# A mixture-of-experts combine brought from a stage of its own into the loops of the next layer

## The chip, the cores and the metric

The kernel runs on one core of a Trainium2 chip. A core has a matrix engine (TensorE, "PE" in the profile, with its weight loads shown as "PEld"), and the engines VectorE (DVE), ScalarE (ACT) and GpSimd (POOL), each of which takes its own instructions in the order in which they were issued to it; SyncE (SP) mostly issues DMAs. The engines wait for each other through semaphores. The metric is the device time of one execution in microseconds (us).

## The reference, cut to what matters

Everything is float32. `x` has 4 sequences of 1024 tokens of 128 features, 4096 tokens in all. Six layers follow one another, each on a layer norm of `x` and added to `x`:

```python
x = x + 0.5 * moe(layernorm(x), wg, w1, b1, w2, b2)
x = x + mamba(layernorm(x), W_in, conv_w, conv_b, W_xproj, W_dt, b_dt, A_log, D, W_out)
x = x + 0.5 * moe(layernorm(x), wg, w1, b1, w2, b2)        # same weights
x = x + 0.5 * soft(layernorm(x), phi_w, phi_b, expert_w, expert_b)
x = x + gla(layernorm(x), Wq, Wk, Wv, Wo, Wf1, Wf2, Wg1, Wg2, norm_weight)
x = x + 0.5 * soft(layernorm(x), phi_w, phi_b, expert_w, expert_b)
```

The first two kinds of layer and the soft one are, in short:

```python
def moe(x):                       # 8 experts of 128 -> 512 -> 128, two of them per token, room for 1024 rows each
    gates_k, idx_k = top_k(softmax(x @ wg), 2); gates_k /= sum(gates_k)
    disp[idx_k, loc] = x          # loc: the token's place in its expert's queue; beyond 1024 it is dropped
    out = relu(disp @ w1 + b1) @ w2 + b2
    return sum_k gates_k * valid * out[idx_k, loc]

def mamba(x):                     # 256 channels, 16 states
    u, z = split(x @ W_in); uc = silu(causal_conv4(u))
    dt, B, C = split(uc @ W_xproj); delta = softplus(dt @ W_dt + b_dt)
    h_t = exp(delta * A) * h_{t-1} + delta * B * uc        # along the tokens of a sequence
    return ((sum_n h * C + uc * D) * silu(z)) @ W_out

def soft(x):                      # 64 experts x 32 slots
    logits = x @ phi.T + phi_b
    D, C = softmax(logits over slots), softmax(logits over experts)
    X = tanh(layernorm(sum_tokens D * x))
    return sum_{experts, slots} C * (X @ expert_w + expert_b)
```

## The kernel before, in words

`x` stays in SBUF for the whole kernel, as 32 tiles of 128 tokens by 128 features. The kernel is one instruction stream per engine. Inside the layers the loops are written under a manual schedule for PE, DVE, ACT and POOL: on each of these engines the instructions stand in exactly the order in which the code issues them. A generator that is stepped with `next` once per turn of a loop is how one piece of work is laid between the pieces of another. Pools of tiles set when a buffer may be filled again.

**Layer norms.** Statistics of four tiles (`ln_stats`, L121 to L123, DVE: eight small instructions and `rstd`, the variance plus epsilon), the power -0.5 (`ln_root`, L130, POOL), the product of minus mean and rstd (`nmr`, L133, DVE), and for each tile `ln_apply` (L143, ACT), which writes the normed tile `xn`.

**The MoE layers** (`moe_layer`, from L148) route the tokens, gather rows of `xn` for the experts in blocks of 512, run the two matmuls, add `b2` (`eo`, L393, DVE), and scatter the result rows into `y2_d` in DRAM by POOL's indirect DMAs (L352), with a small `spacer` memset (L412) between the last ones. Each of a token's two rows has a place of its own in `y2_d`. At the end, the *combine* (L421 to L436) brings them back: for each of eight groups of four tiles, two loads of 256 KB (L425, on SP's queue, three buffers `y`), four scalings by the first gate on ACT (L427), four multiply-adds by the second gate onto `x` on DVE (L431), and one DVE add of 128x512 (L435). `after(j)` is called for each group behind it: the statistics, the power and `nmr` of the next layer's norm.

**Before Mamba** `soft_weights` (L740 to L786) loads the soft layers' `phi`, folds it, and computes on the chip a `flag` that says whether the logits are bounded. Then `mamba_layer` loads its weights on ACT's DMA queue (L456 to L463), `cw` (the convolution's weights times `w_in`, DVE) last.

**Mamba's loop.** A sequence is worked in two halves of 512 tokens, eight halves in all. A half's `prologue` (a generator of 16 steps) norms its four tiles, transposes them (L499, copy L501), computes the convolution and the projections (`pu` L520, silu L531, `dbc` L543, `pd` L565), and softplus (ACT L570 to L575, `w`, `l`, `delta`, `du` on DVE L576 to L580). The loop then runs over 128 units, one for each half and state n; a unit fetches B and C of its state (`fetch`: `Cs` L595 and `Bs` L601 by SP's DMAs, or `pb` by a matmul, L607), multiplies `dBu` (`feed` L617, two units ahead, POOL for ten of the 16 states and DVE for the other six), takes `dA` (`decay` L625, ACT, two ahead), scans two channels' halves along the tokens (`scan` L635, DVE, `hst`), keeps the last column for the next half (`keep` L646, ACT), multiplies by C (`times_c` L651, POOL, `hc`), and sums over the states on PE (`sums` L666). The prologue of the half after the running one is stepped once per unit, from two units before the running half begins to its unit 13. The half before is ended by `epilogue`, stepped from unit 2 on (`zs` L673 DVE, `po` L678 PE, `x` L685 DVE, then the next norm's statistics).

**Before the soft layer** the second MoE's combine is followed by the run-time branch on `flag` (`values_load` L1572, `If` L1573); inside the taken side `phiM` (a copy of the folded `phi` on ACT, L1576, whose last row is set to -1 by a DMA, L1579) is made, and `soft_bounded` begins with a memset of `xT`'s last rows on POOL (L832, `xT` holds all normed tokens transposed).

**The soft layer's first loop** runs over 64 units, half of the 2048 slots by one tile of tokens each. `norm` and `turn`/`take` (L852 transposes into `pt`, which takes a buffer of the logits; L857 copy to `xT` by ACT) prepare the next four tiles, at units 0 to 3 and 4 of each eight. A unit computes logits `l` (L866, PE), their negated maximum `nmh` (L870, DVE), the exponential `ex` (L875, ACT), and one unit later sums and reciprocal (`sm` L882 and L883, DVE) and the weighted `dm` (L887, POOL), and three units later the spread `px` (L898, PE):

```python
for k in range(NK + CS * NB + XL + 3):
    if k < NK:
        logits(k); expo(k)
        g, r = divmod(k, 8)
        if 4 * (g + 1) < NT:
            if r < 4: norm(4 * (g + 1) + r)
            elif r == 4: turn(g + 1); take(g + 1)
    ...
    if 0 <= k - 1 < NK: total(k - 1); weigh(k - 1)
    if 0 <= k - LAG < NK: spread(k - LAG)
```

After this loop come the slots' own work (L924 to L962) and a second loop over combine weights (`clogits` L977 to `finish` L1033), whose `L` buffers come from the pool `lp` of 15.

## Time and profile before

| | us |
| --- | --- |
| median of 3 runs (lowest, highest) | 2390.34 (2389.11, 2394.69) |
| the profiled execution: its time, its span | 2391.2, 2389.1 |
| mean granted clock of PE in it | 0.903 |
| first MoE's last scatter; first loads of `y` | 269.35; 270.8 |
| first convolution matmul of Mamba | 313.1 |
| Mamba's loop, about (one half) | 344 to 889 (67.6) |
| second MoE's last scatter; first loads of `y` | 1157.4; 1158.8 |
| first soft layer's first logits; first `nmh` | 1200.07; 1203.89 |
| its first loop ends, about (eight units of it) | 1429 (28.54) |

The time of an execution is some 2 us above the span that the profile shows of it, and steps of the text are made against that one execution. In the profile's rows, a line number belongs to the code of that kernel; `out<-in` are the program's names; a group's row has the number of instructions, the busy time of all and the mean time of one in ns, and behind the second bar the idle time of that engine just ahead of them with what ended it. A line of the timeline has the start in us, the duration, the engine, the line, the instruction, and in square brackets how long the engine had been idle before it, and for whom it waited.

### The profile page before, as it was taken

Reading aid. Unit: us, or ns where it says so; the run is one execution under the profiler, and the core shown is the slowest. Engines: PE = TensorE matmul, PEld = TensorE weight load, DVE = VectorE, ACT = ScalarE, POOL = GpSimd, SP = SyncE. Lnnn points to the kernel's source line nnn. Section 1 sums busy time; section 2 is a strip of 40 time slices with the busy share of each in tenths; the row PEclk is TensorE's granted clock in tenths of the full one; section 3 lists DMA queues with packets and bytes.
Section 4 is the critical chain, followed back from the end, with each engine's and each line's share of the span. In section 5 each row is a group of like instructions: output and inputs, shape, how many; then the busy total and the mean of one; then the engine's idle time right before and its main releaser. Section 6 shows DMA issues by size and latency. Waiting matters only on the chain. (4 is left out here: it accounts for less than half of the span.)

```text
span 2389.1 us, 17980 instructions
## 1 busy us (share of the span) xinstructions
PE 1959.0 (82%) x5889; PEld 913.7 (38%) x5889; DVE 1391.7 (58%) x1947; ACT 924.2 (39%) x1453; POOL 1392.5 (58%) x898
## 2 busy tenths in 40 slices
PE   4667548899888874687389998999888799989998
PEld 3445313333333233454234444444222344434443
DVE  4211447878779774111477774556688677764444
ACT  3222346566446533222333334333344233334331
POOL 2666328888779881666345556666244355556663
PEclk9989868999978895789699999999898699999999
DMA  6111323232232324111200000000000000000000
GB/s 238 33 44 45 91 100 111 92 115 84 94 107 94 109 78 162 37 46 44 86 1 0 0 1 1 1 1 0 6 0 1 1 0 0 1 1 5 9 9 15
DMA packets 63677, 111.23 MB, mean 47 GB/s; under 512 B 7999, under 2 KB 41423, under 8 KB 58581
## 3 DMA queue, kind: packets, MB, share of 16 engines
q1 hardware_dynamic: 45062, 81.37, 10.3%
q0 software_dynamic: 8192, 16.79, 2.5%
q10 hardware_dynamic: 10322, 11.85, 1.5%
q8 instruction: 48, 0.79, 0.1%
q14 instruction: 53, 0.43, 0.1%
HBM read 90.53 MB, written 19.44 MB: 46 GB/s over the span
## 5 line engine op out<-in xcount | busy, mean ns | idle before, releaser
L887 POOL TENSOR_TENSOR dm<-ex,sm 128x1024 f32<-128x1024 f32 x128 | 244.7, 1913 | 218.2 <-DVE sm L883 125.1
L651 POOL TENSOR_TENSOR hc<-hst,Cs 128x1024 f32<-128x1024 f32 x128 | 278.1, 2183 | 89.8 <-DVE hst L635 41.8
L666 PE MATMUL py<-hc,ident 128*128 128x512 f32 x512 | 287.1, 697 | 38.3 <-POOL hc L651 28.3
L995 POOL TENSOR_TENSOR acc<-acc,L 128x1024 f32<-128x1024 f32 x96 | 226.0, 2354 | 114.4 <-ACT L L987 113.7
L987 ACT ACTIVATE L<-pl,pbc 128x512 f32<-128x512 f32 x256 | 162.1, 684 | 282.3 <-PE pl L977 277.8
L866 PE MATMUL l<-phiT,xT 128*128 128x512 f32 x512 | 246.6, 605 | 14.8 <-ACT xT L857 8.7
L875 ACT ACTIVATE ex<-l,nmh 128x1024 f32<-128x1024 f32 x128 | 142.8, 1115 | 285.4 <-DVE nmh L870 283.4
L977 PE MATMUL pl<-xT,phiM 128*128 128x512 f32 x512 | 242.2, 597 | 0.0
L1021 PE MATMUL py<-L,yt 128*128 128x512 f32 x512 | 238.4, 593 | 4.4 <-DVE L L1011 4.4
L898 PE MATMUL px<-dm,xn 128*128 128x512 f32 x512 | 240.8, 593 | 0.9 <-POOL dm L887 0.9
L870 DVE TENSOR_REDUCE nmh<-l 128x1 f32<-128x1024 f32 x128 | 156.5, 1223 | 107.9 <-PE l L866 107.9
L625 ACT ACTIVATE dA<-delta,A 128x512 f32<-128x512 f32 x256 | 178.4, 721 | 86.3 <-DVE hst L635 83.6
L617 POOL TENSOR_TENSOR dBu<-du,Bs 128x1024 f32<-128x1024 f32 x80 | 177.0, 2214 | 38.0 <-ACT dA L625 38.0
L378 ACT ACTIVATE hT<-ph,cols 128x512 f32<-128x512 f32 x128 | 84.2, 686 | 285.7 <-PE ph L374 166.8
L374 PE MATMUL ph<-dT,w 128*128 128x512 f32 x256 | 137.4, 655 | 69.1 <-ACT hT L378 58.3
L666 PEld LDWEIGHTS py<-hc,ident 128*128 128x128 f32 x512 | 100.9, 211 | 215.2 <-issue 131.2
L352 POOL DMA_INDIRECT y_d<-eo,dest x128 | 126.1, 985 | 92.7 <-DVE eo L393 61.8
L635 DVE TENSOR_TENSOR_SCAN hst<-dA,carry,dBu 128x512 f32<-128x512 f32 x128 | 154.6, 1262 | 5.4 <-POOL dBu L617 4.3
L882 DVE TENSOR_REDUCE sm<-ex 128x32 f32<-128x1024 f32 x128 | 154.7, 1209 | 0.0
L866 PEld LDWEIGHTS l<-phiT,xT 128*128 128x128 f32 x512 | 97.2, 193 | 145.9 <-issue 115.5
L635 DVE TENSOR_TENSOR_SCAN hst<-dA,dBu 128x512 f32<-128x512 f32 x128 | 146.9, 1202 | 6.9 <-ACT dA L625 3.6
L1011 DVE TENSOR_TENSOR L<-L,rd 128x1024 f32<-128x1024 f32 x128 | 147.0, 1211 | 0.1
(248 smaller groups left out, 2856.9 us busy)
## 6 DMA issues: line engine op xcount, KB each, us to landing
Cs<-bc_d SPq DMA_DIRECT2D x32, 1024.0 KB
Bs<-bc_d SPq DMA_DIRECT2D x80, 256.0 KB, 3.3
w<-in_w SPq DMA_DIRECT2D x4, 2048.0 KB
y<-y_d SPq DMA_DIRECT2D x32, 256.0 KB, 3.5
y_d<-zero SPq DMA_DIRECT2D x1, 4096.0 KB
ew<-in_ew ACTq DMA_DIRECT2D x1, 4096.0 KB
x<-in_x SPq DMA_DIRECT2D x8, 256.0 KB, 8.3
xn_da<-xn ACTq DMA_DIRECT2D x8, 256.0 KB, 14.7
```

What stands on the lines that cost most here:

```text
L617: eng.tensor_tensor(dBu, r["du"], r.pop(("B", n)).unsqueeze(2).to_broadcast([P, HB, NC]), ALU.mult,)
L625: nc.scalar.activation(dA, r["delta"][:, :, c], AF.Exp, scale=A[:, c * DS + n : c * DS + n + 1],)
L635: nc.vector.tensor_tensor_scan(hst[:, :, c], r.pop(("dA", n, c)), dBu[:, :, c], 0.0 if h == 0 else carry[b][:, c, n : n + 1], ALU.mult, AL ...
L651: nc.gpsimd.tensor_tensor(hc, r.pop(("h", n)), Cs.unsqueeze(2).to_broadcast([P, HB, NC]), ALU.mult)
L666: nc.tensor.matmul(r["py"][:, c, :], ident, hc[:, :, c], start=False, stop=(n == DS - 1))
L866: nc.tensor.matmul(l[:, q * 512 : (q + 1) * 512], xT[:, j * P : (j + 1) * P], phiN[:, o : o + 512], start=True, stop=True,)
L887: nc.gpsimd.tensor_tensor(dms[k], exs.pop(k), sms.pop(k).unsqueeze(2).to_broadcast([P, NG, PS]), ALU.mult,)
L898: nc.tensor.matmul(px[hf * 2 + q], xns[j // 4][:, j % 4, :], dmf[:, q * 512 : (q + 1) * 512], start=(j == 0), stop=(j == NT - 1),)
L977: nc.tensor.matmul(pl[:, i, :], phiM[:, (2 * c + i) * P : (2 * c + i + 1) * P], xT[:, t * TB : (t + 1) * TB], start=True, stop=True,)
L987: nc.scalar.activation(L[:, i, :], pl[:, i, :], AF.Exp, bias=pbc[:, 2 * c + i : 2 * c + i + 1], scale=-1.0,)
L995: nc.gpsimd.tensor_tensor(accs[t], accs[t], L, ALU.add)
L1021: nc.tensor.matmul(pys[t], yt[:, 2 * c + i, :], L[:, i, :], start=(c + i == 0), stop=(c == CS - 1 and i == 1),)
```

## The change

The combine is taken out of `moe_layer`. The gates are kept in two tiles of the whole kernel, and the combine of one group of four tiles becomes a generator of six steps: the two loads; ACT's four scalings; DVE's four multiply-adds and the add; the statistics; POOL's power; `nmr`. `ln_root` is split into the last two. The `y` buffers are two instead of three.

- For Mamba, group 0 is run ahead of the first prologue and group 1 behind it. From then on, at unit 3 of each of the first six halves, the group of the half after the next is begun (`k // 16 + 2`), and one step of it is issued at the head of each unit, ahead of the epilogue's step. So the loads are issued at unit 3, ACT's scalings at 4, DVE's part at 5, statistics at 6, the power at 7 and `nmr` at 8.
- For the first soft layer, group 0 runs ahead of the first norm and group 1 behind the first `take`; groups 2 to 7 are begun at `k % 8 == 1`, so the loads stand at the head of unit 1 of eight, the scalings at 2, DVE's part at 3, statistics at 4, the power at 5 and `nmr` at 6.
- The branch on `flag` now stands behind the second MoE's scatters and ahead of its combine, and `phiM` is made before the second MoE. On the side of the branch that isn't taken here, the combine runs as a plain loop.
- `lp` has 14 buffers instead of 15.

```diff
+    def ln_pow(ln, j0, n=4):
+        js = slice(j0, j0 + n)
+        nc.gpsimd.tensor_tensor(
+            ln[1][:, js], ln[1][:, js], half_t.to_broadcast([P, n]), ALU.pow
+        )
+
+    def ln_minus(ln, j0, n=4):
         mv, rstd, nmr = ln
         js = slice(j0, j0 + n)
-        nc.gpsimd.tensor_tensor(
-            rstd[:, js], rstd[:, js], half_t.to_broadcast([P, n]), ALU.pow
-        )
         nc.vector.scalar_tensor_tensor(
             nmr[:, js], mv[:, js, 0], -1.0, rstd[:, js], ALU.mult, ALU.mult
         )
+
+    def ln_root(ln, j0, n=4):
+        ln_pow(ln, j0, n)
+        ln_minus(ln, j0, n)
...
-    def moe_layer(w1, w2, b2, tag, ln, after):
+    def moe_layer(w1, w2, b2, tag, ln, gate):
...
-            gate = rp.tile([P, K, NT], F32, name="gate")
...
-                yp = s1.enter_context(tc.tile_pool(name=f"ey{tag}", bufs=3))
...
-                y_v = y2_d[: K * T, :].rearrange("(k j p) d -> p k j d", k=K, p=P)
-                for j in range(0, NT, 4):
...
-                    after(j)
...
+    def combine(yp, gate, j, ln):
...
+        y_v = y2_d[: K * T, :].rearrange("(k j p) d -> p k j d", k=K, p=P)
+        y = yp.tile([P, K, 4, D], F32, name="y")
+        for k in range(K):
+            nc.sync.dma_start(out=y[:, k, :, :], in_=y_v[:, k, j : j + 4, :])
+        yield
+        for i in range(4):
+            nc.scalar.activation(
+                y[:, 0, i, :], y[:, 0, i, :], AF.Copy,
+                scale=gate[:, 0, j + i : j + i + 1],
+            )
+        yield
+        for i in range(4):
+            nc.vector.scalar_tensor_tensor(
+                y[:, 1, i, :], y[:, 1, i, :], gate[:, 1, j + i : j + i + 1],
+                x[:, j + i, :], ALU.mult, ALU.add,
+            )
+        nc.vector.tensor_tensor(
+            x[:, j : j + 4, :], y[:, 0, :, :], y[:, 1, :, :], ALU.add
+        )
+        yield
+        ln_stats(ln, j)
+        yield
+        ln_pow(ln, j)
+        yield
+        ln_minus(ln, j)
+        yield
+
+    def run(pieces):
+        for _ in pieces:
+            pass
...
-    def mamba_layer(ln, ln_next):
+    def mamba_layer(ln, ln_next, before):
...
             with tc.manual_schedule(engines=ENGINES):
-
-                for _ in prologue(*halves[0], rs[0], psa, "dA"):
-                    pass
+                run(before(0))
+
+                run(prologue(*halves[0], rs[0], psa, "dA"))
+                run(before(NJ))
                 for k in range(3):
                     at(fetch, k)
...
-                ahead, behind = iter(()), iter(())
+                ahead, behind, first = iter(()), iter(()), iter(())
                 for k in range(-LEAD, len(units) + 7):
+                    if k % DS == 3 and (k // DS + 2) < len(rs):
+                        first = before((k // DS + 2) * NJ)
+                    if k >= 0:
+                        next(first, None)
                     if k % DS == DS - LEAD and (k + LEAD) // DS + 1 < len(rs):
                         i = (k + LEAD) // DS + 1
                         ahead = prologue(*halves[i], rs[i])
...
-    def soft_bounded(phiN, phiM, pbc, ew, eb, tag, ln, after=None, last=False):
+    def soft_bounded(phiN, phiM, pbc, ew, eb, tag, ln, before=None, after=None, last=False):
...
-            lp = s.enter_context(tc.tile_pool(name=f"slp{tag}", bufs=15))
+            lp = s.enter_context(tc.tile_pool(name=f"slp{tag}", bufs=14))
...
             with tc.manual_schedule(engines=ENGINES):
+                first = iter(())
+                if before:
+                    run(before(0))
                 for i in range(4):
                     norm(i)
                 turn(0)
                 take(0)
+                if before:
+                    run(before(4))
                 for k in range(NK + CS * NB + XL + 3):
+                    if before and k % 8 == 1 and (k // 8 + 2) * 4 < NT:
+                        first = before((k // 8 + 2) * 4)
+                    next(first, None)
                     if k < NK:
                         logits(k)
                         expo(k)
...
     lns = [ln_begin(i) for i in range(6)]
+    gates = [const.tile([P, K, NT], F32, name=f"gate{i}") for i in range(2)]
...
-    moe("a", lns[0], lambda j: ln_group(lns[1], j))
+    moe("a", lns[0], gates[0])
     spool = ctx.enter_context(tc.tile_pool(name="softw", bufs=1, side="right"))
     phiN, pbc, flag = soft_weights(spool)
-    mamba_layer(lns[1], lns[2])
+    with tc.tile_pool(name="ya", bufs=2) as yp:
+        mamba_layer(lns[1], lns[2], lambda j: combine(yp, gates[0], j, lns[1]))
...
     ew, eb = expert_weights(spool2)
+    phiM = spool2.tile([D, NS], F32, name="phiM")
+    nc.scalar.copy(phiM, phiN)
+    mone = spool2.tile([1, 512], F32, name="mone")
+    nc.vector.memset(mone, -1.0)
+    nc.sync.dma_start(
+        out=phiM[D - 1 : D, :].rearrange("o (r c) -> o r c", c=512),
+        in_=mone.unsqueeze(1).to_broadcast([1, NS // 512, 512]),
+    )
...
-    moe("b", lns[2], lambda j: ln_group(lns[3], j))
-
-    def rest(soft):
-        soft("a", lns[3], lambda j: ln_group(lns[4], j))
+    moe("b", lns[2], gates[1])
+
+    def behind_soft(soft):
         gla_layer(lns[4], lns[5])
...
     bounded = nc.values_load(flag, min_val=0, max_val=1)
     with tc.If(bounded > 0) as cmp:
-        with tc.tile_pool(name="softm", bufs=1) as pool:
-            phiM = pool.tile([D, NS], F32, name="phiM")
...
-            rest(lambda *a_, **k: soft_bounded(phiN, phiM, pbc, ew, eb, *a_, **k))
+        def soft(*a_, **k_):
+            soft_bounded(phiN, phiM, pbc, ew, eb, *a_, **k_)
+        with tc.tile_pool(name="yb", bufs=2) as yp:
+            soft("a", lns[3], lambda j: combine(yp, gates[1], j, lns[3]), after)
+        behind_soft(soft)
     with cmp.Else():
...
         nc.scalar.activation(phiN, phiN, AF.Copy, scale=-1.0)
-        rest(lambda *a_, **k: soft_layer(phiN, ew, eb, *a_, **k))
+        with tc.tile_pool(name="yc", bufs=2) as yp:
+            for j in range(0, NT, 4):
+                run(combine(yp, gates[1], j, lns[3]))
+        soft("a", lns[3], after=after)
+        behind_soft(soft)
```

More of the change, by code (lines that the diff above doesn't have):

```diff
@@ L125, in ln_stats @@
         )
-    def ln_root(ln, j0, n=4):
+    def ln_pow(ln, j0, n=4):
[4 more added lines that the diff above has]
+    def ln_minus(ln, j0, n=4):
         mv, rstd, nmr = ln
         js = slice(j0, j0 + n)
-        nc.gpsimd.tensor_tensor(
-            rstd[:, js], rstd[:, js], half_t.to_broadcast([P, n]), ALU.pow
-        )
         nc.vector.scalar_tensor_tensor(
@@ L418, in moe_layer @@
                             output(blk)
-                y_v = y2_d[: K * T, :].rearrange("(k j p) d -> p k j d", k=K, p=P)
-                for j in range(0, NT, 4):
-                    y = yp.tile([P, K, 4, D], F32, name="y")
-                    for k in range(K):
-                        nc.sync.dma_start(out=y[:, k, :, :], in_=y_v[:, k, j : j + 4, :])
-                    for i in range(4):
-                        nc.scalar.activation(
-                            y[:, 0, i, :], y[:, 0, i, :], AF.Copy,
-                            scale=gate[:, 0, j + i : j + i + 1],
-                        )
-                        nc.vector.scalar_tensor_tensor(
-                            y[:, 1, i, :], y[:, 1, i, :], gate[:, 1, j + i : j + i + 1],
-                            x[:, j + i, :], ALU.mult, ALU.add,
-                        )
-                    nc.vector.tensor_tensor(
-                        x[:, j : j + 4, :], y[:, 0, :, :], y[:, 1, :, :], ALU.add
-                    )
-                    after(j)
-    def mamba_layer(ln, ln_next):
+    def combine(yp, gate, j, ln):
[29 more added lines that the diff above has]
+    def mamba_layer(ln, ln_next, before):
         HB = 512
@@ L1536, in gla_layer, with moe @@
                     next(behind, None)
-    def moe(tag, ln, after):
+    def moe(tag, ln, gate):
         with ExitStack() as s:
@@ L1547, in moe @@
             )
-            moe_layer(w1, w2, b2, tag, ln, after)
+            moe_layer(w1, w2, b2, tag, ln, gate)
     lns = [ln_begin(i) for i in range(6)]
+    gates = [const.tile([P, K, NT], F32, name=f"gate{i}") for i in range(2)]
     for j in range(0, NT, 4):
         ln_group(lns[0], j)
-    moe("a", lns[0], lambda j: ln_group(lns[1], j))
+    moe("a", lns[0], gates[0])
     spool = ctx.enter_context(tc.tile_pool(name="softw", bufs=1, side="right"))
     phiN, pbc, flag = soft_weights(spool)
-    mamba_layer(lns[1], lns[2])
+    with tc.tile_pool(name="ya", bufs=2) as yp:
+        mamba_layer(lns[1], lns[2], lambda j: combine(yp, gates[0], j, lns[1]))
     spool2 = ctx.enter_context(tc.tile_pool(name="softw2", bufs=1, side="right"))
     ew, eb = expert_weights(spool2)
+    phiM = spool2.tile([D, NS], F32, name="phiM")
[6 more added lines that the diff above has]
+    )
     for j in range(0, NT, 16):
         ln_root(lns[2], j, 16)
-    moe("b", lns[2], lambda j: ln_group(lns[3], j))
-    def rest(soft):
-        soft("a", lns[3], lambda j: ln_group(lns[4], j))
+    moe("b", lns[2], gates[1])
+    def behind_soft(soft):
         gla_layer(lns[4], lns[5])
@@ L1570, in rest, with after, soft @@
         soft("b", lns[5], last=True)
+    def after(j):
+        ln_group(lns[4], j)
     bounded = nc.values_load(flag, min_val=0, max_val=1)
     with tc.If(bounded > 0) as cmp:
-        with tc.tile_pool(name="softm", bufs=1) as pool:
-            phiM = pool.tile([D, NS], F32, name="phiM")
-            nc.scalar.copy(phiM, phiN)
-            mone = pool.tile([1, 512], F32, name="mone")
-            nc.vector.memset(mone, -1.0)
-            nc.sync.dma_start(
-                out=phiM[D - 1 : D, :].rearrange("o (r c) -> o r c", c=512),
-                in_=mone.unsqueeze(1).to_broadcast([1, NS // 512, 512]),
-            )
-            rest(lambda *a_, **k: soft_bounded(phiN, phiM, pbc, ew, eb, *a_, **k))
+        def soft(*a_, **k_):
[3 more added lines that the diff above has]
+        behind_soft(soft)
     with cmp.Else():
+        def soft(*a_, **k_):
+            soft_layer(phiN, ew, eb, *a_, **k_)
         nc.scalar.activation(phiN, phiN, AF.Copy, scale=-1.0)
-        rest(lambda *a_, **k: soft_layer(phiN, ew, eb, *a_, **k))
+        with tc.tile_pool(name="yc", bufs=2) as yp:
[3 more added lines that the diff above has]
+        behind_soft(soft)
 def kernel(**inputs):
```

## The prediction

> **What bounds the kernel now.** I read the summary first, then busy time by stretches around the four places that the change touches, then the instructions there in order of time, engine by engine, and last the grouped DVE rows of Mamba's loop.
>
> ```profile
> span 2389.1 us, 17980 instructions
> PE 1959.0 (82%) x5889; PEld 913.7 (38%) x5889; DVE 1391.7 (58%) x1947; ACT 924.2 (39%) x1453; POOL 1392.5 (58%) x898
> ...
> 264.00:306.00 42.00, 8.64 (x19) 3.34 (x19) 28.98 (x128) 14.53 (x42) 12.68 (x16) 0.68 0.38 107
> 480.00:550.00 70.00, 61.14 (x131) 23.03 (x131) 56.32 (x56) 42.55 (x74) 58.72 (x30) 0.91 0.29 102
> 1158.00:1200.00 42.00, 1.58 (x4) 0.73 (x4) 26.87 (x123) 14.22 (x38) 12.28 (x9) 0.50 0.35 101
> 1200.00:1300.00 100.00, 97.83 (x229) 42.60 (x230) 73.89 (x82) 38.76 (x48) 50.13 (x27) 0.98 0.00 1
> ```
>
> The columns of a stretch are its length, the busy time of PE, PE's weight loads, DVE, ACT and POOL, the granted clock, and DMA. The shares of the whole run hide the point: in the two stretches of 42 us PE does almost nothing, and the experts' results are combined, on DVE. In Mamba's loop (480 to 550) PE, DVE and POOL are all near 80 to 90%, so none is free. In the soft layer's first loop PE is full and DVE has a quarter of its time left.
>
> Mamba's loop, DVE and then ACT, where the pieces will land:
>
> ```profile
> 500.33 1.22 DVE L617 TENSOR_TENSOR dBu<-du,pb 128x1024 f32<-128x1024 f32 x1 [6.34 <-PE pb L607]
> 501.47 0.68 DVE L685 TENSOR_TENSOR x<-x,po 128x512 f32<-128x512 f32 x1
> 502.06 2.33 DVE L635 TENSOR_TENSOR_SCAN hst<-dA,dBu 128x512 f32<-128x512 f32 x2
> ...
> 506.58 2.32 DVE L635 TENSOR_TENSOR_SCAN hst<-dA,dBu 128x512 f32<-128x512 f32 x2
> ...
> 508.93 0.19 ACT L646 COPY carry<-hst 128x2 f32<-128x2 f32 x1 [2.26 <-DVE hst L635]
> ...
> 531.62 1.77 DVE L576 SCALAR_TENSOR_TENSOR w<-w,e 128x1024 f32<-128x1024 f32 x1 [4.20 <-ACT l L575]
> ```
>
> DVE waits 6.34 us for PE, then runs without a gap up to the scan that ends at 508.9; ACT waits for that scan and is then busy almost without a gap up to `l`, for which DVE waits again. So what is put on DVE between 501.5 and 506.6 lengthens the half.
>
> The soft loop, at the one unit in eight that transposes the next four tiles:
>
> ```profile
> 1242.04 0.35 DVE L883 RECIPROCAL sm<-sm 128x32 f32<-128x32 f32 x1
> 1242.89 0.60 PE L852 MATMUL pt<-ident,xn 128*128 128x128 f32 x4
> 1243.09 1.22 DVE L870 TENSOR_REDUCE nmh<-l 128x1 f32<-128x1024 f32 x1 [0.70 <-PE l L866]
> 1244.41 1.11 ACT L875 ACTIVATE ex<-l,nmh 128x1024 f32<-128x1024 f32 x1 [1.94 <-DVE nmh L870]
> 1245.58 1.98 PE L866 MATMUL l<-phiT,xT 128*128 128x512 f32 x4 [0.37 <-ACT ex L875]
> ```
>
> `pt` takes one of the two buffers of `l`, so the next logits wait for this unit's `ex`: PE has no slack here (it already waits 0.37), and DVE has 0.70 us.
>
> Grouped DVE rows of Mamba's loop, mean ns after the comma:
>
> ```profile
> L579 DVE TENSOR_TENSOR delta<-delta,l 128x1024 f32<-128x1024 f32 x8 | 22.4, 2802 | 0.3
> L576 DVE SCALAR_TENSOR_TENSOR w<-w,e 128x1024 f32<-128x1024 f32 x7 | 17.3, 2473 | 20.9 <-ACT l L575 20.9
> L123 DVE TENSOR_SCALAR rstd<-mv 128x4 f32<-128x4 f32 x7 | 6.6, 949 | 0.2
> L133 DVE SCALAR_TENSOR_TENSOR nmr<-mv,rstd 128x16 f32<-128x16 f32 x1 | 2.1, 2097 | 2.7 <-POOL rstd L130 2.7
> ```
>
> Alone (POOL idle) the first two take 1.23 us, the last two 0.16. Beside a POOL tensor operation they take up to 3.1 us, and the POOL one 2.9 to 3.1 instead of 2.13; one of the two stands until the other ends. Operations with one operand in PSUM (L617, L685), scans and statistics keep their time.
>
> **The change part by part.** Sums are made against the profiled execution, 2391.2 us (span 2389.1 and 2.1 around it); the median of the runs is 2390.34, 0.9 lower.
>
> *First combine taken out.* Before, Mamba's first convolution matmul starts at 313.1, behind all eight groups and then the load of `cw`. After, `w_in` and `cw` are issued on ACT's queue before any combine and land under the fold of phi. DVE is through with the fold at 275.2; the rest of the flag and `cw` 2.5, four L431 1.14, the add 0.69, four statistics pairs 1.67 (their length in Mamba's loop), rstd 0.16, pow 1.07, nmr 0.16 end at 282.7; xn, transposes and copy, about 2.9 as at 1191.7, give 285.6. That is -27.5. The second group now stands between the prologue's `du` and the first feed: 1.14 + 0.69 + 1.67 + 0.16 + 1.07 + 0.16 + 0.1 of gaps = 5.0; the next half's xn, which leads PE there, waited 1.4 before, so +3.7. POOL's first dBu is queued right behind that pow and starts before nmr: +2.1 (0 if it does not block). **-21.7.**
>
> *Six pieces in Mamba's loop* (halves 0 to 5). The DMA pair lies early in SP's order and lands in 3.5 us, ACT's four scalings (1.28) lie where ACT waits 4.9 us for PE; if that cover went, 1.28 per half. On DVE, behind the feed at 500.33: four L431 until 502.6, by when POOL's hc (502.42, 2.13) is waiting; the add goes behind it and ends at 505.4 instead of 503.2. The scan of state 5 is 3.85 late. Statistics 1.67; the first rstd waits for hc of state 5 (510.4); the second statistics were there before. The scan of state 6 ends at 514.5, not 508.85: 5.65 late, and with it ACT's chain to `l`. POOL's pow (1.04) fits, because POOL waits for that scan. Half 0 has a wait of 1.13 of ACT for `pd` in the chain, so 4.4. 5 x 5.65 + 4.4 = **+32.7.** Without blocking it is 1.83 + 1.67 + 0.16 = 3.66 per half, 22.0; those are the two ends.
>
> *Second combine taken out.* First nmh at 1203.89. After: loads land at 1161.7 and 1162.5 as now, DVE's add ends at 1164.4, statistics, rstd, pow, nmr 1168.0, xn and transposes 1170.1, copy 1170.8; the memset of xT (3.51), which held that copy until 1199.4, now runs behind the last scatter. The second group's add waits for ACT's scaling behind the copy (1172.1) and ends the group at 1176.2; nmh of unit 0 follows. **-27.7.**
>
> *Six pieces in the soft loop.* Unit 3 of eight: four L431 and the add, 1.83, with POOL's dm (1.91) let in between: 3.9, less the idle 0.70. Unit 4: statistics 1.67, rstd behind dm 2.2 in all, less 0.70. nmh is 4.7 late, the logits of unit 5 too, and PE has nothing to make it up with: 6 x 4.73 = **+28.4.** Without blocking 6 x 2.26 = 13.6.
>
> *The rest, at nothing.* The branch: between pow and the memset that followed it POOL lost 0.1 us, DVE 0.7; it now lies in the 2.8 us wait for the first load. phiM's copy (1.88 on ACT) moves to where ACT waits 9.56 us for the load of `ew`; if that cover went, 1.9. 14 instead of 15 `L` buffers: the mix that frees a buffer stands ahead of the logits that refill it in PE's own order anyway. On SP the loads of y stand in front of Bs loads, waiting for a DVE add that is over well before those buffers are free; if not, a dBu comes 3.3 late.
>
> The sum is -21.7 + 32.7 - 27.7 + 28.4 = +11.7: 2402.9 for a profiled execution, 2402 for the median.
>
> [...]
>
> **The rivals.**
>
> 1. *Faster: POOL doesn't get in between.* If DVE's operations follow each other too closely, only their own length counts: -23.8 + 22.0 - 27.7 + 13.6 = -15.9, 2374. For it: back to back, L431 overlap by 0.06. Against it: the add depends on the last of them, and between the dependent L578 and L579 POOL did get in (3.03 for L579).
> 2. *One loop blocks, the other not*: -3.1 or -1.1, 2387 to 2389.
> 3. *All hidden*: -23.8 - 27.7 = -51.5, 2339. DVE's idle shares speak for it, the two chains above against it.
> 4. *Much slower: PE's clock drops in each soft wait.* After a wait of 4.36 us in Mamba's loop four matmuls took 3.62 instead of 1.72; at 1200 about ten ran at half speed. 4 to 10 matmuls at 0.43 more, six times: +10 to +26, 2412 to 2428. It decides if the two waits join to more than about 4 us.
>
> That the pieces are not in the loops is excluded: the built order of the queues has them there.
>
> **How the numbers follow.** My forecast 0.50, rival 1 0.15, rival 2 0.15, rival 3 0.05, rival 4 0.15. Within 0.3% is 7.2 us, about what a measurement of this kernel can tell. The forecast's own range is 2394 to 2410, so a fifth of it is "same"; rival 2 nearly all; rivals 1 and 3 are faster, 4 slower: faster 0.23, same 0.22, slower 0.55. The range 2374 to 2420 leaves out rival 3 and the far halves of 1 and 4, some 0.2. A fast and a slow side both hold much; the two entries (each within 3 us) are surer than the two loops.
>
> **What would show it.** The first convolution matmul near 286 and soft's first nmh near 1176 less what Mamba gives back; halves 0 to 5 of Mamba 4 to 6 us longer each, 6 and 7 unchanged; the combine's add and rstd in the loops at 1 to 3 us; a wait of PE for `ex` of 2 to 5 us once per eight soft units, six times; soft b and the GLA layer unchanged. I am wrong if the halves keep their length, or if the add takes 0.7 us in the loops.

## The result, and the profile after

The changed kernel takes 2419.78 us (median of 4 runs, 2414.93 to 2423.44), the kernel before 2392.52 in the runs beside it: ratio 1.0109, 95% interval 1.0089 to 1.0130. Run again on another occasion it took 2417.67 against 2390.66, ratio 1.0115 (1.0098 to 1.0132). So it is 27 us slower; 2402 was forecast, and the range ended at 2420. The profiled execution took 2423.4.

The summary, and the same four stretches as before (columns as there):

```profile
span 2421.4 us, 17953 instructions
PE 1981.6 (82%) x5889; PEld 920.4 (38%) x5889; DVE 1429.8 (59%) x1947; ACT 922.0 (38%) x1453; POOL 1389.6 (57%) x898
...
264.00:306.00 42.00, 23.51 (x45) 9.33 (x46) 12.24 (x37) 12.24 (x23) 5.57 (x11) 0.78 0.24 68
480.00:550.00 70.00, 58.59 (x123) 22.33 (x122) 56.15 (x65) 37.80 (x67) 53.54 (x27) 0.89 0.33 106
1158.00:1200.00 42.00, 24.26 (x131) 16.98 (x130) 10.45 (x31) 12.53 (x25) 21.73 (x33) 0.79 0.21 63
1200.00:1300.00 100.00, 86.94 (x193) 36.69 (x192) 79.67 (x123) 36.12 (x51) 46.39 (x26) 0.94 0.07 21
```

The first of the two stretches in which PE did almost nothing is filled (8.64 us busy became 23.51). The third row of the four, 1158 to 1200, isn't the same stage any more: Mamba's loop is longer, so the second MoE still runs there, up to 1184.3. The idle stretch itself, from the end of the last scatter to the first `nmh`, has shrunk instead, from 46.52 us to 18.27 (before, then after):

```profile
1157.37:1203.89 46.52, 5.40 (x9) 2.49 (x10) 26.87 (x123) 14.24 (x38) 12.28 (x9) 0.50 0.32 92
```

```profile
1184.30:1202.57 18.27, 6.48 (x10) 2.92 (x11) 7.26 (x30) 4.68 (x13) 5.56 (x4) 0.50 0.40 118
```

In their place PE lost 11 of 100 us in the soft loop, and the three busy engines of Mamba's loop all have a little less work in 70 us: the loop runs slower.

By stages, read off the starts of a few instructions (the last scatter of each MoE layer, Mamba's first scan, its last `zs`, the first `nmh`, the first clamp `xs` of the slots, and the last add onto `x`):

| us | before, two profiles | changed, two profiles | difference of the means | forecast |
| --- | --- | --- | --- | --- |
| first MoE's last scatter to Mamba's first scan | 78.7, 80.7 | 63.0, 62.9 | -16.8 | -21.7 |
| first scan to Mamba's last `zs` | 541.9, 542.0 | 580.6, 574.5 | +35.6 | +32.7 |
| from there to the second MoE's last scatter | 267.4, 269.0 | 271.0, 272.1 | +3.4 | 0 |
| from there to the first `nmh` | 47.5, 46.2 | 19.2, 19.2 | -27.6 | -27.7 |
| from there to the first `xs` (soft loop) | 231.9, 231.7 | 264.4, 263.3 | +32.1 | +28.4 |
| from there to the last add onto `x` | 948.5, 948.0 | 949.6, 949.3 | +1.2 | 0 |

The sum of the differences is +27.9. Seven profiles with the changed order in Mamba's loop, those of the experiments among them, lie between 571.9 and 583.6 for its row, so a few us between two such profiles say nothing in that row.

Mamba's loop in the changed kernel, in order of time, the same half as in the fence of before:

```profile
500.88 1.22 DVE L637 TENSOR_TENSOR dBu<-du,pb 128x1024 f32<-128x1024 f32 x1 [6.34 <-PE pb L627]
502.02 1.14 DVE L440 SCALAR_TENSOR_TENSOR y<-y,gate,x 128x128 f32<-128x128 f32 x4
502.97 2.16 POOL L671 TENSOR_TENSOR hc<-hst,Cs 128x1024 f32<-128x1024 f32 x1 [6.40 <-PE py L686]
503.24 2.43 DVE L444 TENSOR_TENSOR x<-y 128x512 f32<-128x512 f32 x1
505.60 0.67 DVE L705 TENSOR_TENSOR x<-x,po 128x512 f32<-128x512 f32 x1
...
506.42 2.04 PE L546 MATMUL pu<-xT,w_in 128*128 128x512 f32 x2 [3.58 <-DVE x L705]
...
511.94 1.18 DVE L123 TENSOR_SCALAR rstd<-mv 128x4 f32<-128x4 f32 x1
513.04 2.32 DVE L655 TENSOR_TENSOR_SCAN hst<-dA,dBu 128x512 f32<-128x512 f32 x2
...
515.39 0.19 ACT L666 COPY carry<-hst 128x2 f32<-128x2 f32 x1 [3.08 <-DVE hst L655]
...
518.64 1.12 DVE L136 SCALAR_TENSOR_TENSOR nmr<-mv,rstd 128x4 f32<-128x4 f32 x1
...
538.07 1.61 DVE L596 SCALAR_TENSOR_TENSOR w<-w,e 128x1024 f32<-128x1024 f32 x1 [4.36 <-ACT l L595]
```

The feed is 0.55 late against before. `hc` slips in ahead of the add, which ends at 505.67; `carry`, which ACT does at the end of the scan of state 6, comes at 515.39 instead of 508.93, 5.9 us later after those 0.55, and `w` is 5.9 later too. Of the detail, the first `rstd` was not held (0.17 us), the second was (1.18); `nmr` was held for 1 us; and PE waited 3.58 us for the late `x` at 506.42, because `po` holds the buffer of the next `pu`; the two matmuls behind that wait took 2.04 instead of 1.10.

The grouped DVE rows of the loop (344 to 890 us), mean ns after the comma:

```profile
L596 DVE SCALAR_TENSOR_TENSOR w<-w,e 128x1024 f32<-128x1024 f32 x7 | 24.2, 3454 | 25.0 <-ACT l L595 25.0
L444 DVE TENSOR_TENSOR x<-y 128x512 f32<-128x512 f32 x6 | 14.6, 2436 | 0.5
L123 DVE TENSOR_SCALAR rstd<-mv 128x4 f32<-128x4 f32 x13 | 11.3, 872 | 0.5
L136 DVE SCALAR_TENSOR_TENSOR nmr<-mv,rstd 128x4 f32<-128x4 f32 x6 | 5.4, 905 | 0.0
```

All six adds took 2.4 us, where one alone takes 0.69. And `w`, a bystander, rose from 2473 to 3454 ns, presumably because a half that is later meets POOL's work at another point; no run separates that.

The soft loop, the units 3 to 5 of eight (their lines of before are in the prediction):

```profile
1242.16 2.69 DVE L440 SCALAR_TENSOR_TENSOR y<-y,gate,x 128x128 f32<-128x128 f32 x4
1242.38 2.06 POOL L912 TENSOR_TENSOR dm<-ex,sm 128x1024 f32<-128x1024 f32 x1 [1.52 <-ACT xn L150]
1244.94 0.69 DVE L444 TENSOR_TENSOR x<-y 128x512 f32<-128x512 f32 x1
1245.55 1.22 DVE L895 TENSOR_REDUCE nmh<-l 128x1 f32<-128x1024 f32 x1
1246.86 1.11 ACT L900 ACTIVATE ex<-l,nmh 128x1024 f32<-128x1024 f32 x1 [4.55 <-DVE nmh L895]
1248.03 0.71 PE L877 MATMUL pt<-ident,xn 128*128 128x128 f32 x4 [1.70 <-ACT ex L900]
...
1252.74 2.90 PE L891 MATMUL l<-phiT,xT 128*128 128x512 f32 x4 [2.29 <-ACT ex L900]
...
1255.69 1.23 DVE L895 TENSOR_REDUCE nmh<-l 128x1 f32<-128x1024 f32 x1 [2.69 <-PE l L891]
```

`dm` gets in among the four multiply-adds, which take 2.69 us instead of 1.14; `nmh` is late, `pt` waits 1.70 for `ex`, the next logits 2.29, and then run slowly, 2.90 us for four instead of 1.98. Eight units, counted from one `pt` to the next, take 34.13 us where that happens and 28.54 before.

The slow matmuls are PE's clock. In the profiles of before and of the changed kernel the granted clock is either 1.00 or 0.50, and every stretch at one of the two, but the last, is 3.41 us long or a whole multiple of that. In this soft loop it is at 0.50 for one such slot in each turn, from 1216.12, 1253.66, 1287.80, 1321.93, 1356.06 and 1390.20. Three slots around the turn above in this profile, and four around a turn of the second profile with the same two waits (1.70 and 2.29 us, ending at 1243.89 and 1248.60); the clock is the third number from the end of a row:

```profile
1246.83:1250.25 3.42, 2.22 (x8) 1.05 (x8) 3.21 (x11) 1.50 (x2) 1.83 (x1) 1.00 0.51 147
1250.25:1253.66 3.41, 1.12 (x3) 0.49 (x3) 2.71 (x4) 1.59 (x2) 0.60 (x2) 1.00 0.01 2
1253.66:1257.07 3.41, 3.41 (x5) 1.33 (x4) 1.38 (x2) 0.06 (x1) 2.35 (x2) 0.50 0.00 0
```

```profile
1240.72:1244.13 3.41, 1.71 (x6) 0.63 (x5) 3.30 (x5) 1.41 (x2) 0.00 (x0) 1.00 0.40 118
1244.13:1247.55 3.42, 2.18 (x8) 0.81 (x6) 3.25 (x12) 0.20 (x2) 1.91 (x1) 1.00 0.12 36
1247.55:1250.96 3.41, 2.36 (x6) 1.16 (x7) 1.61 (x3) 1.48 (x2) 1.96 (x2) 1.00 0.01 2
1250.96:1254.37 3.41, 3.41 (x10) 1.50 (x9) 2.70 (x5) 1.12 (x1) 1.78 (x2) 1.00 0.00 0
```

In the first, the whole second wait lies in one slot, in which PE is idle for 2.29 us, and the next slot runs at 0.50. In the second, an edge at 1247.55 cuts that wait in two, no slot is idle for more than 1.70, and the clock stays at 1.00: from that `pt` eight units take 32.44 us. So the second wait alone was enough where it lay within one slot, and was not where an edge cut it. In the soft loop of the first profile a slot at 0.50 followed on each of the six slots with 2.29 to 2.89 us of idle PE and on none with 1.32 or less; in that of before no slot had more than 1.53, and from 1204.29 on the clock was 1.00. The changed kernel's low slots come in all six turns of the one profile and in five of the other; the first turn, with a wait of 3.16 us, is one of them.

At Mamba's entry, SP's queue before and then after:

```profile
270.82 3.24 SPq L425 DMA_DIRECT2D y<-y_d  x6
275.35 0.34 SPq L785 DMA_DIRECT2D pb_d<-pb  x1
```

```profile
276.75 0.34 SPq L810 DMA_DIRECT2D pb_d<-pb  x1
278.21 0.28 SPq L811 DMA_DIRECT2D phiT<-pb_d  x1
278.70 7.04 SPq L431 DMA_DIRECT2D y<-y_d  x6
...
281.81 1.28 ACT L434 ACTIVATE y<-y,gate 128x128 f32<-128x128 f32 x4 [5.08 <-DMA y<-y_d]
```

The first loads of `y` used to be issued ahead of the two small DMAs of the fold of `phi`. Now they stand behind them, and those wait for the fold: 8 us later, 278.70 instead of 270.82.

### The profile page after: what moved, and what is told of

Same layout as the page of the kernel before. It is cut to its first block, busy times and chain, and to the rows that moved or that the text cites. A ratio compares the mean times of both kernels' runs of the same rounds, so it can differ in the third digit from the quotient of the medians.

```text
span 2421.4 us, 17953 instructions
## 1 busy us (share of the span) xinstructions
PE 1981.6 (82%) x5889; PEld 920.4 (38%) x5889; DVE 1429.8 (59%) x1947; ACT 922.0 (38%) x1453; POOL 1389.6 (57%) x898
## 5 line engine op out<-in xcount | busy, mean ns | idle before, releaser
L923 PE MATMUL px<-dm,xn 128*128 128x512 f32 x512 | 246.6, 604 | 0.4 <-POOL dm L912 0.4
```

The source lines that it names most:

```text
L923: nc.tensor.matmul(px[hf * 2 + q], xns[j // 4][:, j % 4, :], dmf[:, q * 512 : (q + 1) * 512], start=(j == 0), stop=(j == NT - 1),)
```

## The experiments

Each kernel is the changed one with the edit shown. Times compare with the kernel before run beside it on the same chip; that took about 2390 us on some occasions and about 2338 on others (on record, chips 0 and 2 for the first, 6 and 1 for the second, each on one occasion). In the profiles that difference lies in the two MoE layers, some 30 us in each (for instance 242 instead of 271 us from Mamba's last `zs` to the second MoE's last scatter); what makes it was not tried. The entries and the soft loop are alike within 1 or 2 us where the code is the same, and are compared across; Mamba's loop in the changed order spreads as said above.

**One part at a time.** The second combine as one stage again:

```diff
+    with tc.tile_pool(name="yb", bufs=3) as yp:
+        for j in range(0, NT, 4):
+            run(combine(yp, gates[1], j, lns[3]))
...
-            soft("a", lns[3], lambda j: combine(yp, gates[1], j, lns[3]), after)
+        soft("a", lns[3], after=after)
```

> Only the first combine is in pieces (Mamba's loop); the second is one stage again ahead of the branch, as before. Theory 'two independent bills': the profile of the changed kernel, read by stages, gave Mamba's entry -15.4 us, its eight halves +38.6, the second MoE +3.7, the soft entry -28.3 and the soft loop +32.6. Undoing the second part must then leave -15.4 + 38.6 = +23 us against the kernel before (2413 to 2418; +27 if the second MoE's 3.7 belong to the copy of phi, which this kernel keeps early). Rival 'shared cause' (the branch's place, 14 buffers, or the early phi copy make a good part of the loss): the time stays within 5 us of the changed kernel's 2420 although the soft loop is as before.

And the first one as one stage again:

```diff
     moe("a", lns[0], gates[0])
+    with tc.tile_pool(name="ya", bufs=3) as yp:
+        for j in range(0, NT, 4):
+            run(combine(yp, gates[0], j, lns[1]))
...
-        mamba_layer(lns[1], lns[2], lambda j: combine(yp, gates[0], j, lns[1]))
+    mamba_layer(lns[1], lns[2], lambda j: iter(()))
```

> Only the second combine is in pieces (soft layer's loop); the first is one stage again. Two independent bills: soft entry -28.3, soft loop +32.6, so +4 us against before, +8 with the second MoE's 3.7: 2394 to 2402, and Mamba's halves 67 to 69 us again. Rival 'shared cause': more than +15 us. The half of Mamba that took 77.4 us in the profile of before, at a clock of 0.82, decides another thing: if it is there in this profile too, it is a property of the order of before, if not, of that one execution.

Mamba's part alone: 2357.84 against 2337.09, +20.8 where +23 was expected, ratio 1.0096 (1.0073 to 1.0118); the soft stages are back at 46.5 and 232.8. This kernel keeps the 14 `L` buffers, so they cost 1.0 us at most in that loop. The soft part alone: 2351.62, +14.5, ratio 1.0062 (1.0041 to 1.0083), where 4 to 8 was expected. The excess is at Mamba's entry, which took 88.0 us, 8.3 more than the 79.7 of before: in this kernel the fold of `phi` doesn't run beside the combine as it did before, but behind it (its matmuls start at 273.93, 4 us behind the last add of the combine). So its one-stage entry is not that of before; without those 8.3 it is +6.2. The two bills then make 20.8 + 6.2 = 27.0, and no sign of a shared cause is left.

**Before and changed, profiled on one chip.**

> The kernel before, for a profile on the chip of the other runs. Two points are open. Half 4 of Mamba: 77.4 us in the profile of before and 77.4 to 78.7 in every other one, so it is expected at 77 again (a property of the program); if it comes out at 68, the profile of before was a single bad draw and the loop's bill is 9 us higher than read. The second MoE, from Mamba's last zs to its last scatter: 241 to 243 in the four kernels that copy phi early, on that chip. Theory 'the copy of phi delays it by 3.7': 237 to 239 here. Rival 'drift of the DMAs': 240 to 243 here too.

> The changed kernel against the kernel before on the chip of the other runs. The four kernels run so far give, in differences to before: first part alone +20.8, second part alone +14.5 (of which 9.2 is its one stage entry, which stands worse than before's), so the two bills say 20.8 + 14.5 - 9.2 = +26 us. Rival (the parts interact): more than 5 us away from that.

The first took 2389.85. Half 4 of Mamba takes 77.5 us again, its neighbours 68: it is a property of that order, and that half has room for a piece (77.5 and 78.7 in the changed kernel, where the halves 1, 2, 3 and 5 pay 6.6 to 9.4). The changed kernel took 2417.67 against 2390.66, +27.0, where 26 had been worked out. The second MoE took 269.0 in the one and 272.1 in the other. The figures of 237 to 243 that were set for it came from occasions of the 2338 kind and can't be compared with these; more on that below.

**Mamba's pieces elsewhere.**

```diff
-                    if k % DS == 3 and (k // DS + 2) < len(rs):
+                    if k % DS == 1 and (k // DS + 2) < len(rs):
                         first = before((k // DS + 2) * NJ)
-                    if k >= 0:
-                        next(first, None)
+                    if k >= 0 and k % DS in (1, 3, 5):
+                        next(first, None)
+                        if k % DS == 5:
+                            next(first, None)
...
                     at(scan, k)
+                    if k >= 0 and k % DS == 4:
+                        next(first, None)
+                        next(first, None)
                     at(keep, k)
```

> As the changed kernel, but Mamba's pieces stand where DVE waits: loads at the head of unit 1, ACT's scalings at 3, DVE's multiply-adds, add and statistics behind the scan of unit 4, which is ahead of the feed that waits 5 to 6.3 us for PE, and the power and nmr at the head of unit 5. Theory 'place' (the cost came because the pieces stood behind that wait, on the way to ACT's chain): halves 0 to 5 fall from 75 to 77 us to 68 to 69, 35 to 45 us less than the changed kernel: 2375 to 2385, faster than before. In the gap POOL's hc may still hold the add for up to 2 us, which the gap takes. Theory 'work' (DVE is near full in the loop, and 3.7 us more per half lengthen it wherever they stand): the halves stay at 72 us or more, 2400 or more.

2330.66 against 2337.09, ratio 0.9975 (0.9960 to 0.9991), in place of +27. The halves 1 to 6 are 68.3, 68.5, 68.2, 77.5, 68.4, 67.6 (67.9, 68.3, 68.0, 77.5, 68.3, 67.6 before), and the loop 543.6 us against 542 before. The same instructions cost 35.6 us in one place and under 2 in another. The timeline of DVE and POOL in one half:

```profile
452.48 3.25 DVE L440 SCALAR_TENSOR_TENSOR y<-y,gate,x 128x128 f32<-128x128 f32 x4
452.88 2.19 POOL L671 TENSOR_TENSOR hc<-hst,Cs 128x1024 f32<-128x1024 f32 x1
455.83 0.69 DVE L444 TENSOR_TENSOR x<-y 128x512 f32<-128x512 f32 x1
...
458.90 1.22 DVE L637 TENSOR_TENSOR dBu<-du,pb 128x1024 f32<-128x1024 f32 x1 [0.44 <-PE pb L627]
460.03 0.15 DVE L136 SCALAR_TENSOR_TENSOR nmr<-mv,rstd 128x4 f32<-128x4 f32 x1
```

POOL gets in here as well (3.25 us for four multiply-adds), but the feed's wait for PE, 6.34 us in the changed kernel, absorbs all of it, and 0.44 is left. The theory 'work' is out.

**The soft layer's pieces, place and collision.** Two units later:

```diff
-                    if before and k % 8 == 1 and (k // 8 + 2) * 4 < NT:
+                    if before and k % 8 == 3 and (k // 8 + 2) * 4 < NT:
```

> As the changed kernel, but the soft layer's pieces begin two units later: loads at unit 3 of eight, scalings at 4, DVE's multiply-adds and add at 5, statistics at 6, the power at 7, nmr at the head of unit 8. They then stand behind the unit that turns the next four tiles instead of ahead of it and in it. Theory 'place' (the turn takes a buffer of the logits, so that only there a late maximum holds PE at once; elsewhere DVE may be 2 us late and makes up 0.7 us a unit): eight units fall from 34.1 to 29 to 30.5 us, 20 to 30 us less in all: 2390 to 2400. Theory 'work' (each microsecond of DVE lost to the piece or to POOL is lost to PE wherever it stands): 32 to 34 us for eight units, at most 10 us less than the changed kernel.

Same units, but between the unit's sum and its reciprocal:

```diff
+            def total(k, pieces=iter(())):
                 sm = sms[k] = wk.tile([P, NG], F32, name="sm")
                 nc.vector.tensor_reduce(sm, exs[k], AX.X, ALU.add)
+                next(pieces, None)
                 nc.vector.reciprocal(sm, sm)
...
-                    next(first, None)
+                    if k % 8 in (1, 2, 5):
+                        next(first, None)
...
-                        total(k - 1)
+                        total(k - 1, first if k % 8 in (3, 4, 6) else iter(()))
```

> The changed kernel with the soft layer's whole pieces in the same two units (3 and 4 of eight), but on DVE between a unit's sum and its reciprocal, where POOL waits for that reciprocal: place as in the changed kernel, no collision with POOL. With the run two units later (collision, good place: 30.35 us for eight units) it makes the four cases whole. Theory 'both count, and the clock is a follower of the long waits': 30.5 to 31.5 us for eight units (the 1.83 and 1.67 us less 0.70 of idle time each, and no or hardly any matmul at the low clock). Theory 'the collision alone': 29 or less. Theory 'the place alone': 33 or more.

The same, begun a unit earlier, so that against the changed kernel the piece and the reciprocal just ahead of it change places:

```diff
-                    if before and k % 8 == 1 and (k // 8 + 2) * 4 < NT:
+                    if before and k % 8 == 0 and (k // 8 + 2) * 4 < NT:
...
+                    if k % 8 in (0, 1, 5):
+                        next(first, None)
...
+                        total(k - 1, first if k > 1 and k % 8 in (2, 3, 6) else iter(()))
```

> The run before with whole pieces between sum and reciprocal gave 29.35 us for eight units, but it also put each piece behind the next maximum instead of ahead of it, so it moved place and collision at once. Here one thing alone is changed against the changed kernel: the reciprocal of the unit and the piece behind it change their order on DVE (the loads and scalings go one unit earlier for that). The pieces delay the same two maxima as in the changed kernel, only POOL's dm starts behind them instead of between. Theory 'collision': without it the piece costs its own 1.83 and 1.67 us less 0.70 of idle time each, 2.1 to 2.3, and PE's waits are too short for the low clock: 30.6 to 30.9 us for eight units. Rival 'place': 33 or more, as in the changed kernel (34.1). Rival 'slack': 29.5 or less, if PE rides out delays of 1.1 us.

And cut to units, none in the unit that turns, all between sum and reciprocal:

```diff
+    def combine_fine(yp, gate, j, ln):
...
+        for i in range(4):
+            nc.vector.scalar_tensor_tensor(
+                y[:, 1, i, :], y[:, 1, i, :], gate[:, 1, j + i : j + i + 1],
+                x[:, j + i, :], ALU.mult, ALU.add,
+            )
+            nc.vector.tensor_tensor(x[:, j + i, :], y[:, 0, i, :], y[:, 1, i, :], ALU.add)
+            yield
...
+                        for o in (0, 1, 8):
+                            heads.setdefault(s0 + o, []).append(gg)
+                        for o in (2, 3, 4, 5, 6, 7, 11):
+                            mids_.setdefault(s0 + o, []).append(gg)
```

> The changed kernel with the soft layer's pieces cut to one tile (multiply-add and add) or two tiles' statistics per unit, none in the unit that turns, and put on DVE between a unit's sum and its reciprocal: POOL waits for that reciprocal then, so that neither can hold the other, and no piece is longer than about 1 us. Theory 'place and lock': eight units at 28.6 to 29.2 us (28.5 before, 34.1 changed, 30.4 with the whole pieces two units later), 29 to 33 us less than the changed kernel, -6 to 0 against before. Theory 'work': DVE's 3.7 us per eight units don't fit into its idle 0.7 us per unit less the turn's, and eight units stay at 30.4 or more.

| | eight units, us (from `pt` to `pt`) | loop, us |
| --- | --- | --- |
| before | 28.54 | 231.8 |
| changed, with a low slot behind the second wait | 34.13 | 263.9 |
| changed, the one turn where the clock stays | 32.44 | |
| two units later | 30.35 | 242.0 |
| between sum and reciprocal, behind the next maximum | 29.35 | 236.6 |
| piece and reciprocal swapped | 30.17 | 242.3 |
| cut to units | 28.54 (first one 29.09) | 233.0 |

Two units later is 2336.53 against 2337.09, ratio 0.9999 (0.9984 to 1.0013): 'place', as expected for it. The run between sum and reciprocal (a single run, 2332.05) came out at 29.35, below the 30.5 to 31.5 of the theory that I favoured; it also moves the piece behind one more maximum, so that it couldn't decide. The swap, in which the order of one pair alone is changed, decides between them. Its timeline:

```profile
1269.68 1.13 DVE L440 SCALAR_TENSOR_TENSOR y<-y,gate,x 128x128 f32<-128x128 f32 x4
1270.84 0.69 DVE L444 TENSOR_TENSOR x<-y 128x512 f32<-128x512 f32 x1
1271.45 0.35 DVE L909 RECIPROCAL sm<-sm 128x32 f32<-128x32 f32 x1
1271.71 1.16 DVE L895 TENSOR_REDUCE nmh<-l 128x1 f32<-128x1024 f32 x1
1271.94 1.91 POOL L913 TENSOR_TENSOR dm<-ex,sm 128x1024 f32<-128x1024 f32 x1 [3.17 <-DVE sm L909]
...
1278.39 1.98 PE L891 MATMUL l<-phiT,xT 128*128 128x512 f32 x4 [1.83 <-ACT ex L900]
```

The multiply-adds take 1.13 again, `pt` doesn't wait, the logits wait 1.83 and run at 1.98, and no slow group is left. So of the 5.59 us per eight units, 1.63 are the piece's own length (30.17 - 28.54), 2.27 the collision with POOL (32.44 - 30.17), and 1.69 the low clock behind the longer waits (34.13 - 32.44); a slot of 3.41 us at half the clock loses 1.71. 30.17 lies 0.4 below the range of 'collision', whose sum for the piece's own length, 2.1 to 2.3, was too high, and above what 'slack' allowed; 'place' is out. The split holds for these places alone: two units later POOL gets in as before (the four multiply-adds take 2.70 us there), and eight units still take 30.35, without a low slot. So the place costs too, and the three figures aren't prices to be carried to another place. This was one run and one profile, 2405.70 beside 2394.13, but its six intervals from the first turn on agree within 0.1 us. Cut to units and without either, the loop is 1.2 us longer than before, and the kernel 2386.20 against 2390.66, ratio 0.9979 (0.9967 to 0.9992).

**Mamba's entry.** Pieces in the gap as above, and:

```diff
-                run(prologue(*halves[0], rs[0], psa, "dA"))
-                run(before(NJ))
+                p0 = prologue(*halves[0], rs[0], psa, "dA")
+                for _ in range(3):
+                    next(p0)
+                run(before(NJ))
+                run(p0)
...
+        head = {j: combine(yp, gates[0], j, lns[1]) for j in (0, 4)}
+        for pieces in head.values():
+            next(pieces)
+        phiN, pbc, flag = soft_weights(spool)
...
```

> The kernel with Mamba's pieces in DVE's gap (6.4 us under before), and two changes at Mamba's entry: the first two groups' loads are issued ahead of the folding of phi, so that they don't stand behind its two DMAs on SP's queue, and the second group's combine stands behind the third step of the first prologue, where DVE waits some 25 us, instead of between the prologue's last product and the first feed. Theory: the loads' place cost the first part of the entry (the first scaling at 281.8 though DVE is free at 278.8: 3 to 4 us), and the second group 6.8 us; 10 to 11 us less, -16 to -18 against before. If the first matmul stays where it is, the loads wait for the last scatters and not for the queue, and only 6.8 come off.

2376.35 against 2390.66, ratio 0.9935 (0.9915 to 0.9956), -14.3, a little short of the 16 to 18 expected. From the last scatter to the first scan it takes 51.4 us instead of 62.9: -11.5, where 10 to 11 was expected. The shortfall is in Mamba's loop, 547.1 us in this profile and 543.6 in the one with the gap alone; why is open. The loads are issued at 270.19, four of them ahead of the two DMAs of the fold, the first scaling starts at 273.18 instead of 281.81, and what the first matmul waits for now is `cw`:

```profile
285.32 9.01 PE L540 MATMUL pu<-xT,cw 128*128 128x512 f32 x16 [2.39 <-DVE cw L486]
```

**All together, and the copy of phi.** The gap, the entry and the cut pieces in one kernel; and the same with the copy of `phi`, its memset and its DMA behind the second MoE:

```diff
-    nc.scalar.copy(phiM, phiN)
...
     moe("b", lns[2], gates[1])
+    nc.scalar.copy(phiM, phiN)
```

> Mamba's pieces in DVE's gap, the two changes at Mamba's entry, and the soft layer's pieces cut to units and put between sum and reciprocal, together. The three were measured one by one at -14.3 against before (gap and entry) and -31.5 against the changed kernel (soft); if they add up, -46 us against before: 2341 to 2348 where before takes 2390, ratio 0.979 to 0.983. If the bills interact, at most -35.

> As the kernel before it, but the copy of phi on ACT, its memset and its DMA stand behind the second MoE's tokens on their queues instead of ahead of them. From Mamba's last zs to the MoE's last scatter it took 267.4 and 269.0 us in two profiles of before and 270.1 to 272.2 in four with the early copy. Theory 'the early copy costs': 267 to 269 here, 2 to 3 us less than the kernel with the early copy. Rival 'the loads of the expert weights drift': 270 to 272 in both.

2287.67 against 2338.87, ratio 0.9783 (0.9760 to 0.9807), and 2284.02, ratio 0.9768 (0.9745 to 0.9792): 51 and 55 us faster than before. The gains add up (46 expected). The second MoE takes 242.2 us in the first and 239.5 in the second, and 240.7 to 243.5 in the five others with the early copy where before takes 2338: the early copy costs some 1 to 4 us, by a single profile of the late one. In it ACT's first DMA of `xn` is issued 14.7 us after ACT's load of `ew`, and 15.6 and 14.6 in the two profiles of before; in all eleven with the early copy it is 19.5 to 20.9. Why it slips by more than the copy's 1.90 us, with 4 MB of `ew` and 4 MB of `w` under way, was not tried. The two totals themselves are not told apart by their intervals.

## Why the prediction was right, and where it wasn't

The side was right, the size was not: +27 instead of +11.7. 2417.7 and 2419.8 lie at the upper end of the range and within rival 4, outside the forecast's own 2394 to 2410. That 2419.8 came in 0.2 us below the end of the range is luck: the six rows of the table were off by 4.9, 2.9, 3.4, 0.1, 3.7 and 1.2 us, all to the same side, 16.2 in all. Of the signs that were named, the add at 2.4 us in Mamba's loop and the first `nmh` came true; the first convolution matmul came at 291 and not near 286, and most halves paid more than the 4 to 6 us. Step by step:

- **First combine taken out, -21.7: -16.8.** The step that failed is the fold's end as the start of the first group. The working put the multiply-adds right behind the fold and `cw`, and never priced SP's queue, past which the loads had moved: they are issued at 278.70, and the add ends at 284.8 instead of about 279.5. The run with the loads ahead gave that back: its first convolution matmul starts 17.4 us behind the last scatter instead of 22.3. The second group between `du` and the first feed, and POOL's `dBu` that starts before `nmr`, came as forecast: `nmr` took 2.07, and from `w` to the first scan it takes 13.2 us instead of 6.5, +6.8 against 5.8.
- **Six pieces in Mamba's loop, +32.7: +32.5 and +38.7 in the two pairs.** The mechanism is the forecast's: POOL gets in between the last multiply-add and the add (add ends at 505.67, 505.4 forecast after the 0.55), and the scan of state 6 is 5.9 late (5.65). Two things inside were off and partly cancelled: halves 1, 2, 3 and 5 pay 6.6 to 9.4, and half 4 nothing in the one profile and 1.2 in the other. PE's wait for the late `x` and `w`, which meets POOL later on, lie in those halves; how much each adds was not tried. Half 4's 77.5 us stood in the profile of before and were not read.
- **Second combine taken out, -27.7: -27.6.** Right in its parts: the memset is behind the last scatter, and the first `nmh` waits for the second group.
- **Six pieces in the soft loop, +28.4: +32.1.** The sum per eight units, 4.73, is 3.90 without the clock and 5.59 with it. The mechanism, one entry of POOL per piece, is the forecast's, but both pieces were priced too high: the next maximum is 2.6 us late where 3.2 was forecast (3.9 less 0.70), and the one behind it 1.3 more where it was 1.5. The clock, which the forecast left out, made up for more than that. So the near fit of this row is two errors that cancel in part. Rival 4's drop of the clock came in six turns of the one profile and five of the other, at 1.69 us each behind the wait of 2.29. Its condition, that the two waits join to more than about 4 us, was an estimate of mine from the single wait of 4.36 us, and it was wrong: the waits were 1.70 and 2.29 us with 2.4 us of work between, and behind the second, where it lay within one slot, the clock was 0.50 for 3.41 us.
- **At nothing: the copy of phi.** It was costed by ACT's wait that hides it. The wait is there, but what stands behind the copy on ACT's queue, the DMA of `xn`, was not looked at: it is issued some 5 us later, +1 to +4 in all by the run that moves it.
- **Rivals.** 1 (POOL doesn't get in), 2 (it gets in in one loop only) and 3 (all hidden) fell with both loops as the change has them. But the swap shows rival 1's premise to be in reach of a few lines of code, and the gap in Mamba's loop (under 2 us left) and the cut pieces in the soft one (+1.2) come near rival 3's.

Which DVE instructions were held beside a POOL tensor operation, and which kept their time, the profile of the changed kernel shows: in Mamba's loop the add took 2.43 us (0.69 in the soft loop), the second `rstd` shown above 1.18 (the first 0.17) and `nmr` 1.12 (0.15 in the run with the gap), while the scans stayed at 1.19 to 1.28, DVE's `dBu` from PSUM at 1.19 to 1.22 and the statistics at 0.26 to 0.29 and 0.18. The reductions of the soft loop kept their time, the sums at 1.20 to 1.22 us and the maxima, before and the swap included, at 1.16 to 1.23. For the clock, a slot of 3.41 us with 2.29 us of idle PE in it was enough, so that the slot didn't have to be idle all through.

## What to carry to other kernels

A piece of work laid into a full loop costs by its place more than by its length: behind the wait of its engine it was paid in full and more (35.6 us in Mamba's loop), ahead of it the wait paid (under 2). Before laying it in, look for what the neighbour engine starts on what signal: here the order of one reciprocal and the piece decided whether POOL ran against it. And when a step moves, list what now stands ahead of each of its DMAs on the queue that issues them.

## What was not expected of the hardware

- PE's clock fell to 0.50 for 3.41 us behind a single wait of 2.29 us, where that wait lay within one slot of the clock; the one time that a slot's edge cut it in two the clock stayed at 1.00, and in the swap the four matmuls behind a wait of 1.82 or 1.83 us took 1.98 us, six times out of six.
- POOL gets in among independent DVE instructions too: four multiply-adds took 2.69 and 3.25 us around one `dm` or `hc`, and 1.13 or 1.14 without.
- From one occasion to another, the MoE layers differ by some 30 us each with the same instructions, the soft loop by 1 or 2; whether it is the chip was not tried.
